# A cross-attention and mixture-of-experts layer: how the router's choice of four is computed, and when its steps are issued

## The chip, the core and the metric

The kernel runs on one core of one Trainium2 chip. The core has five engines that each take their instructions in order from a queue of their own and wait for each other by semaphores: TensorE (PE in the profile, with PEld for its weight loads), VectorE (DVE), ScalarE (ACT), GpSimd (POOL) and SyncE (SP, which here only issues DMA transfers). The metric is the device time of one execution in microseconds. The kernel before took 1699.78 us, the median of three runs that went from 1699.21 to 1702.81 us.

## What is computed

A layer on 4 sequences of 512 tokens of width 512: layer norm, cross-attention to a context of 1601 rows (257 image rows and 1344 text rows, two softmaxes, 16 heads), a residual sum, a second layer norm, and a feed-forward part with 32 experts and a shared expert. The change lies in the feed-forward part. Cut to what matters:

```python
scores = sigmoid(x @ router_w.T)                     # T = 2048 tokens, 32 experts
sc = scores + e_bias
group_scores = top_k(sc.reshape(T, 8, 4), 2)[0].sum(-1)
gidx = top_k(group_scores, 3)[1]                     # three of eight groups
masked = where(expert's group is chosen, sc, 0.0)
topk_idx = top_k(masked, 4)[1]                       # the choice of four
topk_w = 2.5 * scores[topk_idx] / (sum of the four + 1e-20)

# each expert takes its first C = 80 tokens, in order of the token number
Y[e] = (silu(Xp[e] @ W_gate[e]) * (Xp[e] @ W_up[e])) @ W_down[e]    # Xp[e]: 80 gathered rows
out[slots_token] += Y * slots_w
shared = silu(x @ shared_gate.T) * (x @ shared_up.T) @ shared_down.T
result = x + out + shared
```

All arrays are float32.

## The kernel before

The order of the work on every engine is written out by hand: a planner has no part in it. An engine that reaches an instruction whose inputs are not there stands still, with all that is queued behind it.

**Stages.** The loop over the four batches `b` computes keys, queries and values, then the attention by groups of four heads (`c` from 0 to 3) and key tiles (`t` from 0 to 12). Inside a batch first come the keys, sixteen chunks of four matmuls (`keys`, L718), then a written-out list with the last scores and the residual steps of the batch before (L793), then the attention. `residual` (L441) projects the attention's output, adds x, normalizes, transposes, and computes the router's logits of 128 tokens.

After the last batch comes the shared expert (`shared`, L938): 32 units of mostly 3.4 us of TensorE work (`gate`, `up` and `down` of 128 x 512 results). Here `residual` of the last batch is spread over units 8 to 15 (`side`). Then come the 32 experts (loop at L1118): `gate_up(e)`, `turn(e + 2)`, `down(e - 1)`, with eight units of the shared expert strewn between, and at the end eight last units.

**The router.** `routing(b, space)` (L511) returns a list of small steps for the 512 tokens of one batch, nearly all on DVE, with 128 tokens on the partitions and four such rows side by side. `carve` lays its small arrays out in a scratch tile `space`. The steps are: the sigmoid on ACT (or by exp, for batches 0 and 1), the bias, the two largest of each group, the rank of each group, the masked scores `cand`; then four rounds that each find the largest left, settle ties by the smaller expert number with the help of `rev` (32, 31, ... 1), and take the hit out (L583 to L597); then the weights and their DMA to `xw_d` (L605), behind the normed rows that the experts gather. Then `ranks` (L611) transposes the 0/1 choice to 32 x 512 on PE, and DVE adds it to `merged`, where each chosen token's key is larger the smaller its number. Nineteen steps of `search` (ten MAX8 and nine match-replaces on 32 x 592 elements, L625 to L629) keep the 80 largest keys of each expert in `best`, over all batches.

**When the steps are issued.** For batches 0 and 1 the steps go two per key tile of the last head group of the next batch (L879 to L886), then seven per key chunk of the batch after it (L789), and the search one per key tile (L877). For batches 2 and 3 they are dealt out in the shared-expert stage by `deal(i)` (L1085): after unit `i`, as many steps as keep a running sum `spent` (0.8 for a search step, 0.3 for another) under `(i - 1) * SHARE`. Batch 2 has its scratch in a tile of its own, `rp` (L1072), batch 3 in a tile that the attention has left (L1105), from unit 16 on (`ready`).

**From the router to the experts.** Before unit 30, the last but one, all steps that are left are issued, and then `tokens` (L929): two DVE steps turn `best` into token numbers (`past`), PE transposes them (L935), DVE casts them to `tok` (L936). Then six `gather(e)` (L1013, `AHEAD`) are issued on POOL's queue: indirect DMAs of 80 rows each into `xp`, a ring of seven buffers. In the expert loop `down(e - 1)` issues its scatter (L1050), which adds to `out`, and then `gather(e + 5)` follows on the same queue. `turn(e)` transposes the gathered rows on PE (L1026) and copies them on DVE (L1028). The expert's weights come by SP's queue into rings of six buffers (`expert_weights`, L919): one expert after every fourth unit, then each as a buffer comes free. SP's queue also holds the loads of x rows for `residual` (L168), of rows for `down` of the shared expert (L977) and all writes.

PSUM is a ring of eight banks, each taken in turn by `psum`.

Of the kernel before, what the change touches and what calls it, by code (L numbers as in the profile page):

```python
# [109 lines left out]
def body(ctx, tc, a, ident, mhalf, logits, x1_d, xw_d, xnT_d, den_d, rec_d, out):  # L110
# [383 lines left out]

    rt = pool("rt", 1)
    e_b = rt.tile([P, E], F32, name="e_b")
    rev = rt.tile([P, 1, E], F32, name="rev")
    below = rt.tile([P, NG, NG], F32, name="below")

    merged = rt.tile([E, CAP + L], F32, name="merged")  # L500
# [1 line left out]

    def routing_constants():
        nc.scalar.dma_start(e_b, a["e_bias"].partition_broadcast(P))
        nc.gpsimd.iota(rev[:, 0, :], [[-1, E]], base=E, channel_multiplier=0, allow_small_or_imprecise_dtypes=True)
        nc.gpsimd.memset(below, 1.0)

        nc.gpsimd.affine_select(below, below, [[1, NG], [-1, NG]], ALU.is_gt, 0.0, base=0, channel_multiplier=0)
        nc.vector.memset(best, 0.0)

    def routing(b, space, by_exp=False):  # L511


        tt, ts, tr = nc.vector.tensor_tensor, nc.vector.tensor_scalar, nc.vector.tensor_reduce
        lo = b * NQ
        taken = []

        def carve(*shape):

            n = NQ  # L520
            for d in shape:
                n *= d
            at = sum(taken)
            taken.append(n)
            names = " ".join("abc"[:len(shape)])
            return space[:, at:at + n].rearrange(
                f"p (t {names}) -> p t {names}", t=NQ, **dict(zip("abc", shape))
            )

        lg = logits[:, lo:lo + NQ, :]  # L530

        both = carve(4 * E)
        first_half, second_half = space[:, :2 * NQ * E], space[:, 2 * NQ * E:4 * NQ * E]
        gt, eq = (x.rearrange("p (t a b) -> p t a b", t=NQ, a=NG) for x in (first_half, second_half))
        cand, hit, sel, chosen = (
            space[:, k * NQ * E:(k + 1) * NQ * E].rearrange("p (t e) -> p t e", t=NQ) for k in range(4)
        )
        sc, sb = carve(E), carve(E)
        m = [carve(NG) for _ in range(4)]
        gs, rank, top = carve(NG), carve(NG), carve(1)  # L540
        g = sb.rearrange("p t (g k) -> p t g k", k=EG)
        one = gs.unsqueeze(3).to_broadcast([P, NQ, NG, NG])
        oth = gs.unsqueeze(2).to_broadcast([P, NQ, NG, NG])
        rv = rev.to_broadcast([P, NQ, E])
        before = below.unsqueeze(1).to_broadcast([P, NQ, NG, NG])

        def wide_(x):
            return x.to_broadcast([P, NQ, E])

        if by_exp:  # L550

            work = [
                lambda: nc.scalar.activation(sc, lg, AF.Exp, scale=-1.0),
                lambda: ts(sc, sc, 1.0, None, ALU.add),
                lambda: nc.vector.reciprocal(sc, sc),
            ]
        else:
            work = [lambda: nc.scalar.activation(sc, lg, AF.Sigmoid)]
        work += [
            lambda: tt(sb, sc, e_b.unsqueeze(1).to_broadcast([P, NQ, E]), ALU.add),  # L560

            lambda: tt(m[0], g[:, :, :, 0], g[:, :, :, 1], ALU.max),
            lambda: tt(m[1], g[:, :, :, 0], g[:, :, :, 1], ALU.min),
            lambda: tt(m[2], g[:, :, :, 2], g[:, :, :, 3], ALU.max),
            lambda: tt(m[3], g[:, :, :, 2], g[:, :, :, 3], ALU.min),
            lambda: tt(m[1], m[1], m[3], ALU.max),
            lambda: tt(m[3], m[0], m[2], ALU.min),
            lambda: tt(m[0], m[0], m[2], ALU.max),
            lambda: tt(m[1], m[1], m[3], ALU.max),
            lambda: tt(gs, m[0], m[1], ALU.add),  # L570

            lambda: tt(gt, oth, one, ALU.is_gt),
            lambda: tt(eq, oth, one, ALU.is_equal),
            lambda: tt(eq, eq, before, ALU.mult),
            lambda: tt(gt, gt, eq, ALU.add),
            lambda: tr(rank, gt, AX.X, ALU.add),
            lambda: ts(rank, rank, float(TKG), None, ALU.is_lt),
            lambda: tt(
                cand.rearrange("p t (g k) -> p t g k", k=EG), g, rank.unsqueeze(3).to_broadcast([P, NQ, NG, EG]), ALU.mult
            ),  # L580
        ]

        for k in range(TOPK):  # L583
            into = sel if k else chosen
            work += [
                lambda: tr(top[:, :, 0], cand, AX.X, ALU.max),
                lambda: tt(hit, cand, wide_(top), ALU.is_equal),
                lambda: tt(hit, hit, rv, ALU.mult),
                lambda: tr(top[:, :, 0], hit, AX.X, ALU.max),
                lambda into=into: tt(into, hit, wide_(top), ALU.is_equal),  # L590
            ]
            if k:
                work.append(lambda: tt(chosen, chosen, sel, ALU.add))
            if k < TOPK - 1:
                work.append(
                    lambda into=into: nc.vector.scalar_tensor_tensor(cand, into, -BIG, cand, ALU.mult, ALU.add)
                )  # L597
        work += [
            lambda: tt(sb, chosen, sc, ALU.mult),
            lambda: tr(top[:, :, 0], sb, AX.X, ALU.add),  # L600
            lambda: ts(top, top, 1e-20, None, ALU.add),
            lambda: nc.vector.reciprocal(top, top),
            lambda: ts(top, top, SCALE_ROUTE, None, ALU.mult),
            lambda: tt(sb, sb, wide_(top), ALU.mult),
            lambda: nc.sync.dma_start(  # L605
                xw_d[lo * P:(lo + NQ) * P, D:].rearrange("(t p) e -> p t e", p=P), sb
            ),
        ]
        key = merged[:, CAP:]

        def ranks():  # L611
            ps = psum()
            for i in range(NQ):
                nc.tensor.transpose(ps[:E, i * P:(i + 1) * P], chosen[:, i, :], ident)  # L614
            nc.vector.scalar_tensor_tensor(key, ps[:E, :], float(T), key, ALU.mult, ALU.add)

        work += [
            lambda: nc.gpsimd.iota(
                key, [[-1, L]], base=T - b * L, channel_multiplier=0, allow_small_or_imprecise_dtypes=True
            ),  # L620
            lambda: nc.vector.tensor_copy(merged[:, :CAP], best),
            ranks,
        ]
        search = []
        for j in range(CAP // 8):  # L625
            at = best[:, 8 * j:8 * j + 8]
            search.append(lambda at=at: nc.vector.max(at, merged))
            if j < CAP // 8 - 1:
                search.append(lambda at=at: nc.vector.match_replace(merged, at, merged, 0.0))  # L629
        return work, search  # L630
# [292 lines left out]
            nc.sync.dma_start(t, a[name][e])  # L923
            weights.setdefault(e, []).append(t)

    SHARE = 2.4
    AHEAD, WEIGHTS = 6, 6

    def tokens():  # L929

        past = ew.tile([E, CAP], F32, name="past", bufs=1)
        nc.vector.tensor_scalar(past, best, T + 0.5, float(T), ALU.is_gt, ALU.mult)
        nc.vector.scalar_tensor_tensor(past, past, float(T), best, ALU.add, ALU.subtract)
        ps = psum()
        nc.tensor.transpose(ps[:CAP, :E], past, ident[:E, :E])  # L935
        nc.vector.tensor_copy(tok, ps[:CAP, :E])  # L936
# [73 lines left out]
    def expert_parts():  # L1010
        weights, xps, xpTs, hs = {}, {}, {}, {}

        def gather(e):  # L1013
            xps[e] = ew.tile([CAP, D + E], F32, name="xp", bufs=AHEAD + 1)
            nc.gpsimd.indirect_dma_start(
                out=xps[e][:, :],
                out_offset=None,
# [51 lines left out]
    early.close()  # L1069
    wgp = pool("wgp", WEIGHTS, side="right", reuse_waits="tile")  # L1070
    ew = pool("ew", 3, side="right", reuse_waits="tile")
    rp = pool("rp", 1, side="right", reuse_waits="tile")  # L1072
    tok = ew.tile([CAP, E], I32, name="tok", bufs=1)
    weights, gather, turn, gate_up, down = expert_parts()
    rest = [residual(B - 1, qt, aoT_last, lambda: wo) for qt in range(NQ)]
    first, second = sum(routing(B - 2, rp.tile([P, 1024], F32, name="space")), []), None
    O_AT = 8
    side = {}
    for qt in range(NQ):
        for i, f in enumerate(rest[qt]):  # L1080
            side.setdefault(O_AT + qt + i, []).append(f)
    ready = O_AT + NQ + 4
    spent = 0.0

    def deal(i):  # L1085

        nonlocal spent
        while spent < (i - 1) * SHARE and (first or second):
            todo = first or second
            spent += 0.8 if len(todo) < 2 * CAP // 8 else 0.3  # L1090
            todo.pop(0)()

    for i, u in enumerate(units):
        if i < 2:
            continue
        if i == len(units) - 2:
            for f in first + second:
                f()
            first, second = [], []
            tokens()  # L1100
            for e in range(AHEAD):
                gather(e)
        if i == ready:

            space = mid.tile([P, 2, L], F32, name="rb")  # L1105
            second = sum(routing(B - 1, space.rearrange("p k t -> p (k t)")), [])
            deal(i)
        u()
        for f in side.get(i, ()):
            f()  # L1110
# [66 lines left out]
```

## Time and profile before

| | us |
|---|---|
| median of three runs | 1699.78 |
| the profiled execution, its own time | 1697.61 |
| its span, from the first to the last instruction | 1695.9 |
| first unit of the shared expert starts on PE | 1324.4 |
| `tokens` on PE (L935) | 1452.0 |
| first expert's matmuls start | 1460.5 |
| last eight units start | 1664.5 |
| record of the last matmul ends | 1692.1 |

The granted clock of PE is 1.00 in all forty slices of the page. The groups of the routing that matter, from the timelines:

| step | on | us for one |
|---|---|---|
| 128x128 elements, as L586 to L596 | DVE | 0.29, starts 0.32 apart |
| 128x32 elements, as L562 to L570 | DVE | 0.19 to 0.22 |
| MAX8 of 32x592, L627 | DVE | 0.76 |
| match-replace of 32x592, L629, with its value load | DVE | 0.75 + 0.07 |
| transposes of a choice, four, L614 | PE | 0.6 together |
| a gather, L1015 | POOL | 0.93, starts 1.21 apart; lands 3.0 to 3.3 later |
| a scatter, L1050 | POOL | 1.42; lands 6.0 later (median) |

How to read the profile: busy times are sums of instruction records. Records of matmuls overlap, since matmuls are pipelined and their ends are modelled. In timelines each line has start, duration, engine, line, operation, output and inputs, and in square brackets how long the engine stood idle before, and what released it. In a list of waits each line has the waiting line, what released it, the total in us, how often, and the longest.

### The profile page before, as it was taken

Reading aid. Unit: us, or ns where it says so; the run is one execution under the profiler, and the core shown is the slowest. Engines: PE = TensorE matmul, PEld = TensorE weight load, DVE = VectorE, ACT = ScalarE, POOL = GpSimd, SP = SyncE. Lnnn points to the kernel's source line nnn. Section 1 sums busy time; section 2 is a strip of 40 time slices with the busy share of each in tenths; the row PEclk is TensorE's granted clock in tenths of the full one; section 3 lists DMA queues with packets and bytes.
Section 4 is the critical chain, followed back from the end, with each engine's and each line's share of the span. In section 5 each row is a group of like instructions: output and inputs, shape, how many; then the busy total and the mean of one; then the engine's idle time right before and its main releaser. Section 6 shows DMA issues by size and latency. Waiting matters only on the chain. (4 is left out here: it accounts for less than half of the span.)

```text
span 1695.9 us, 29514 instructions
## 1 busy us (share of the span) xinstructions
PE 1683.7 (99%) x11773; PEld 885.0 (52%) x11773; DVE 981.1 (58%) x2024; ACT 643.1 (38%) x1370; POOL 868.4 (51%) x614
## 2 busy tenths in 40 slices
PE   9999999999999999999999999999999999999999
PEld 5554444446544444465444445654443344677774
DVE  4765554857655549776665597766655777211111
ACT  2135456611355566114555651145556401111110
POOL 3246977332569764336697643366884210233331
PEclk9999999999999999999999999999999999999999
DMA  7000000321100103120010041210001365599964
GB/s 234 1 1 1 27 27 2 114 67 63 38 1 27 27 2 123 59 72 29 2 27 27 2 147 34 81 44 2 14 15 64 132 206 188 176 287 297 306 179 117
DMA packets 68969, 138.40 MB, mean 82 GB/s; under 512 B 16224, under 2 KB 28640, under 8 KB 66784
## 3 DMA queue, kind: packets, MB, share of 16 engines
q1 hardware_dynamic: 62704, 124.11, 22.1%
q0 software_dynamic: 5120, 10.82, 3.1%
q8 instruction: 93, 1.52, 0.4%
q10 hardware_dynamic: 1008, 1.59, 0.3%
q14 instruction: 44, 0.36, 0.1%
HBM read 113.68 MB, written 22.81 MB: 80 GB/s over the span
## 5 line engine op out<-in xcount | busy, mean ns | idle before, releaser
L372 ACT ACTIVATE pT<-ps 128x512 f32<-128x512 f32 (+1 forms) x832 | 429.7, 603 | 345.9 <-PE ps L371 337.8
L334 DVE TENSOR_REDUCE mx<-ps 128x1 f32<-128x512 f32 (+1 forms) x576 | 331.3, 617 | 265.1 <-PE ps L320 265.1
L387 POOL TENSOR_TENSOR acc<-acc,pT 128x1024 f32<-128x1024 f32 x192 | 445.7, 2360 | 3.0 <-ACT pT L372 2.6
L290 PEld LDWEIGHTS ps<-v_w,cT 128*128 128x128 f32 (+1 forms) x1408 | 168.9, 186 | 102.2 <-DVE mx L334 56.1
L379 PE MATMUL po<-pT,v 128*32 128x512 f32 (+2 forms) x1792 | 222.3, 603 | 0.0
L371 PE MATMUL ps<-qT,kT 32*128 32x512 f32 (+1 forms) x1664 | 213.7, 587 | 0.0
L320 PE MATMUL ps<-kT,qT 32*128 32x512 f32 (+1 forms) x1536 | 206.4, 549 | 0.0
L290 PE MATMUL ps<-v_w,cT 128*128 128x128 f32 (+1 forms) x1408 | 197.7, 284 | 0.0
L231 PE MATMUL ps<-cT,wk 128*128 128x512 f32 (+1 forms) x384 | 154.0, 545 | 0.2 <-DMA wk<-in_k_w 0.2
L308 DVE TENSOR_REDUCE mx<-ps 128x1 f32<-128x512 f32 (+2 forms) x256 | 128.2, 565 | 6.4 <-PE ps L305 6.4
L1050 POOL DMA_INDIRECT out<-y,tok x32 | 45.4, 1420 | 133.2 <-DMA out<-y,tok 72.5
L368 PEld LDWEIGHTS <-pick 32*128 32x128 bf16 (+1 forms) x832 | 21.6, 91 | 165.8 <-issue 164.0
L231 PEld LDWEIGHTS ps<-cT,wk 128*128 128x128 f32 x384 | 69.6, 190 | 70.5 <-issue 55.5
L298 ACT COPY v<-ps 128x128 f32<-128x128 f32 (+1 forms) x208 | 59.7, 287 | 117.7 <-PE ps L290 117.3
L238 POOL TENSOR_TENSOR sq_k<-sq_k,sq 128x512 f32<-128x512 f32 (+2 forms) x48 | 49.6, 1034 | 104.5 <-ACT sq L235 104.1
L1040 DVE TENSOR_TENSOR ehT<-ehT,ps 128x160 f32<-128x160 f32 x32 | 10.3, 321 | 158.3 <-ACT ehT L1039 144.1
L394 POOL TENSOR_TENSOR acc<-pT 128x1024 f32<-128x1024 f32 x24 | 56.1, 2360 | 86.8 <-ACT pT L372 54.3
L387 POOL TENSOR_TENSOR pT<-pT 65x1024 f32<-65x1024 f32 x24 | 56.0, 2355 | 86.8 <-PE po L379 78.1
L320 PEld LDWEIGHTS ps<-kT,qT 32*128 32x128 f32 x1536 | 82.1, 183 | 31.0 <-issue 10.1
L387 DVE TENSOR_TENSOR acc<-acc,pT 128x1024 f32<-128x1024 f32 (+1 forms) x72 | 96.7, 1391 | 2.1 <-ACT pT L372 2.1
L379 PEld LDWEIGHTS po<-pT,v 128*32 128x32 f32 (+2 forms) x1792 | 34.9, 107 | 118.6 <-issue 109.3
L368 PE MATMUL ps<-mT,pick 32*128 32x512 bf16 (+1 forms) x832 | 82.5, 385 | 2.5 <-ACT mT L359 2.5
(244 smaller groups left out, 2194.5 us busy)
## 6 DMA issues: line engine op xcount, KB each, us to landing
W_gate<-in_W_gate SPq DMA_DIRECT2D x32, 512.0 KB
W_up<-in_W_up SPq DMA_DIRECT2D x32, 512.0 KB
W_down<-in_W_down SPq DMA_DIRECT2D x32, 512.0 KB
rb<-rec_d SPq DMA_DIRECT2D x64, 128.0 KB
xt<-in_x SPq DMA_DIRECT2D x30, 256.0 KB
cT<-in_ctxT SPq DMA_DIRECT2D x7, 1024.0 KB
wki<-in_k_img_w SPq DMA_DIRECT2D x4, 1024.0 KB
wo<-in_o_w SPq DMA_DIRECT2D x4, 1024.0 KB
```

Of the source, the lines that this page charges most:

```text
L231: nc.tensor.matmul(ps[:, :n], lhsT=wt[:, k, c * P:(c + 1) * P], rhs=xT[:, k, to], start=k == 0, stop=k == NC - 1)
L290: nc.tensor.matmul(ps[lo:hi, :], lhsT=cTs[bl][:, k, at:at + hi - lo], rhs=ws[bl == NB - 1][:, k, c * P:(c + 1) * P], start=k == 0, stop=k ...
L298: nc.scalar.copy(v[:n, t, :], ps[:n])
L308: nc.vector.tensor_reduce(mx[:, qt, g, bl:bl + 1], ps[:, :n], AX.X, ALU.max, negate=True)
L320: nc.tensor.matmul(ps[:, j * n:(j + 1) * n], lhsT=qT[r:r + HD, c, q * P:(q + 1) * P], rhs=kT[r:r + HD, c, k0:k0 + n], start=True, stop=True,)
L334: nc.vector.tensor_reduce(mx[:, qt, g, i:i + 1], ps[:, :m], AX.X, ALU.max, negate=True)
L368: nc.tensor.matmul(ps[:n], lhsT=pick[r:r + HD, kind(t), :n], rhs=mT[r:r + HD, :], start=True, stop=False)
L371: nc.tensor.matmul(ps[:n], lhsT=kT[r:r + HD, c, t * P:t * P + n], rhs=qT[r:r + HD, c, :], start=False, stop=True)
L372: nc.scalar.activation(pT[:n, g, :], ps[:n], AF.Exp)
L379: nc.tensor.matmul(po[r:r + HD, :], lhsT=v[rows, t, r:r + HD], rhs=pT[rows, g, :], start=start, stop=stop)
L387: (nc.vector if idle else nc.gpsimd).tensor_tensor(to[rows, h, :], to[rows, h, :], pT[rows, h, :], ALU.add)
L394: (nc.vector if idle else nc.gpsimd).tensor_tensor(acc[:, h, :], pTs[0][:, h, :], pTs[1][:, h, :], ALU.add)
```

## The change

1. The four rounds of the choice are replaced. `cand` now lies in rows of 36 (`filled`), the last four of which hold a very low number. For each of the four rows of tokens a MAX8 gives the eight largest of 32; the lower four of these are overwritten by the same low number; a match-replace takes the eight values out of the 36, each once; and a comparison of `cand` with what is left gives the choice. `rev` and its iota are gone.
2. `SHARE` is 2.7 instead of 2.4. In `deal`, when the next step is `ranks` (20 steps left), the dealing stops for this part, once for each batch, so that `ranks` comes with the next part. At unit 16 the running sum is set forward instead of dealing at once.
3. All steps that are left, and the two DVE steps of the slots, are issued before unit 29 (`kept_tokens`); the transpose, the cast and the gathers stay before unit 30.
4. `AHEAD` is 8 instead of 6, and `xp` has `AHEAD` buffers (8) instead of `AHEAD + 1` (7).
5. The scratch of batch 2 is the first buffer of the ring of `W_down`; the tile `rp` is gone.

```diff
--- before.py
+++ after.py
@@ -494,7 +494,6 @@
 
     rt = pool("rt", 1)
     e_b = rt.tile([P, E], F32, name="e_b")
-    rev = rt.tile([P, 1, E], F32, name="rev")
     below = rt.tile([P, NG, NG], F32, name="below")
 
     merged = rt.tile([E, CAP + L], F32, name="merged")
@@ -502,7 +501,6 @@
 
     def routing_constants():
         nc.scalar.dma_start(e_b, a["e_bias"].partition_broadcast(P))
-        nc.gpsimd.iota(rev[:, 0, :], [[-1, E]], base=E, channel_multiplier=0, allow_small_or_imprecise_dtypes=True)
         nc.gpsimd.memset(below, 1.0)
 
         nc.gpsimd.affine_select(below, below, [[1, NG], [-1, NG]], ALU.is_gt, 0.0, base=0, channel_multiplier=0)
@@ -532,16 +530,19 @@
         both = carve(4 * E)
         first_half, second_half = space[:, :2 * NQ * E], space[:, 2 * NQ * E:4 * NQ * E]
         gt, eq = (x.rearrange("p (t a b) -> p t a b", t=NQ, a=NG) for x in (first_half, second_half))
-        cand, hit, sel, chosen = (
-            space[:, k * NQ * E:(k + 1) * NQ * E].rearrange("p (t e) -> p t e", t=NQ) for k in range(4)
+
+        row_ = E + 8 - TOPK
+        filled, rest_ = (
+            space[:, k * NQ * row_:(k + 1) * NQ * row_].rearrange("p (t e) -> p t e", t=NQ) for k in range(2)
         )
+        cand = filled[:, :, :E]
+        chosen = space[:, 2 * NQ * row_:2 * NQ * row_ + NQ * E].rearrange("p (t e) -> p t e", t=NQ)
         sc, sb = carve(E), carve(E)
         m = [carve(NG) for _ in range(4)]
-        gs, rank, top = carve(NG), carve(NG), carve(1)
+        gs, rank, top, largest8 = carve(NG), carve(NG), carve(1), carve(8)
         g = sb.rearrange("p t (g k) -> p t g k", k=EG)
         one = gs.unsqueeze(3).to_broadcast([P, NQ, NG, NG])
         oth = gs.unsqueeze(2).to_broadcast([P, NQ, NG, NG])
-        rv = rev.to_broadcast([P, NQ, E])
         before = below.unsqueeze(1).to_broadcast([P, NQ, NG, NG])
 
         def wide_(x):
@@ -575,26 +576,20 @@
             lambda: tt(gt, gt, eq, ALU.add),
             lambda: tr(rank, gt, AX.X, ALU.add),
             lambda: ts(rank, rank, float(TKG), None, ALU.is_lt),
+            lambda: nc.vector.memset(filled[:, :, E:], -BIG / 2),
             lambda: tt(
                 cand.rearrange("p t (g k) -> p t g k", k=EG), g, rank.unsqueeze(3).to_broadcast([P, NQ, NG, EG]), ALU.mult
             ),
         ]
 
-        for k in range(TOPK):
-            into = sel if k else chosen
-            work += [
-                lambda: tr(top[:, :, 0], cand, AX.X, ALU.max),
-                lambda: tt(hit, cand, wide_(top), ALU.is_equal),
-                lambda: tt(hit, hit, rv, ALU.mult),
-                lambda: tr(top[:, :, 0], hit, AX.X, ALU.max),
-                lambda into=into: tt(into, hit, wide_(top), ALU.is_equal),
-            ]
-            if k:
-                work.append(lambda: tt(chosen, chosen, sel, ALU.add))
-            if k < TOPK - 1:
-                work.append(
-                    lambda into=into: nc.vector.scalar_tensor_tensor(cand, into, -BIG, cand, ALU.mult, ALU.add)
-                )
+
+        work += [lambda t=t: nc.vector.max(largest8[:, t, :], cand[:, t, :]) for t in range(NQ)]
+        work += [lambda: nc.vector.memset(largest8[:, :, TOPK:], -BIG / 2)]
+        work += [
+            lambda t=t: nc.vector.match_replace(rest_[:, t, :], largest8[:, t, :], filled[:, t, :], -BIG)
+            for t in range(NQ)
+        ]
+        work += [lambda: tt(chosen, cand, rest_[:, :, :E], ALU.is_gt)]
         work += [
             lambda: tt(sb, chosen, sc, ALU.mult),
             lambda: tr(top[:, :, 0], sb, AX.X, ALU.add),
@@ -923,14 +918,18 @@
             nc.sync.dma_start(t, a[name][e])
             weights.setdefault(e, []).append(t)
 
-    SHARE = 2.4
-    AHEAD, WEIGHTS = 6, 6
-
-    def tokens():
+    SHARE = 2.7
+    AHEAD, WEIGHTS = 8, 6
+
+    def kept_tokens():
 
         past = ew.tile([E, CAP], F32, name="past", bufs=1)
         nc.vector.tensor_scalar(past, best, T + 0.5, float(T), ALU.is_gt, ALU.mult)
         nc.vector.scalar_tensor_tensor(past, past, float(T), best, ALU.add, ALU.subtract)
+        return past
+
+    def tokens(past):
+
         ps = psum()
         nc.tensor.transpose(ps[:CAP, :E], past, ident[:E, :E])
         nc.vector.tensor_copy(tok, ps[:CAP, :E])
@@ -1011,7 +1010,7 @@
         weights, xps, xpTs, hs = {}, {}, {}, {}
 
         def gather(e):
-            xps[e] = ew.tile([CAP, D + E], F32, name="xp", bufs=AHEAD + 1)
+            xps[e] = ew.tile([CAP, D + E], F32, name="xp", bufs=AHEAD)
             nc.gpsimd.indirect_dma_start(
                 out=xps[e][:, :],
                 out_offset=None,
@@ -1069,42 +1068,50 @@
     early.close()
     wgp = pool("wgp", WEIGHTS, side="right", reuse_waits="tile")
     ew = pool("ew", 3, side="right", reuse_waits="tile")
-    rp = pool("rp", 1, side="right", reuse_waits="tile")
     tok = ew.tile([CAP, E], I32, name="tok", bufs=1)
     weights, gather, turn, gate_up, down = expert_parts()
     rest = [residual(B - 1, qt, aoT_last, lambda: wo) for qt in range(NQ)]
-    first, second = sum(routing(B - 2, rp.tile([P, 1024], F32, name="space")), []), None
+
+    space = wgp.tile([P, NI, D], F32, name="W_down", tag="W_down")
+    first, second = sum(routing(B - 2, space.rearrange("p n d -> p (n d)")), []), None
     O_AT = 8
     side = {}
     for qt in range(NQ):
         for i, f in enumerate(rest[qt]):
             side.setdefault(O_AT + qt + i, []).append(f)
     ready = O_AT + NQ + 4
-    spent = 0.0
+    spent, waited = 0.0, None
+    N_SEARCH = 2 * (CAP // 8) - 1
 
     def deal(i):
 
-        nonlocal spent
+        nonlocal spent, waited
         while spent < (i - 1) * SHARE and (first or second):
             todo = first or second
+            if len(todo) == N_SEARCH + 1 and waited is not todo:
+
+                waited = todo
+                break
             spent += 0.8 if len(todo) < 2 * CAP // 8 else 0.3
             todo.pop(0)()
 
     for i, u in enumerate(units):
         if i < 2:
             continue
-        if i == len(units) - 2:
+        if i == len(units) - 3:
             for f in first + second:
                 f()
             first, second = [], []
-            tokens()
+            past = kept_tokens()
+        if i == len(units) - 2:
+            tokens(past)
             for e in range(AHEAD):
                 gather(e)
         if i == ready:
 
             space = mid.tile([P, 2, L], F32, name="rb")
             second = sum(routing(B - 1, space.rearrange("p k t -> p (k t)")), [])
-            deal(i)
+            spent = (i - 1) * SHARE
         u()
         for f in side.get(i, ()):
             f()
```

## The prediction

> **What bounds the kernel now.** I read the head of the page first, then the list of what TensorE (PE) waited for, then the timelines of PE and VectorE (DVE) around the longest of those waits that lies near the change.
>
> ```profile
> span 1695.9 us, 29514 instructions
> PE 1683.7 (99%) x11773; PEld 885.0 (52%) x11773; DVE 981.1 (58%) x2024; ACT 643.1 (38%) x1370; POOL 868.4 (51%) x614
> ```
>
> PE has 1683.7 us of records in 1695.9 us, so 12.2 us at most stand open. The list of PE's waits names 8.3 us of them; nearly all the rest is the tail behind the last matmul (its record ends at 1692.1).
>
> ```profile
> PE ps L368 <- ACT mT L359: 2.5, 4, 0.6
> PE ps L468 <- DVE xn L220: 1.8, 3, 0.6
> PE ps L639 <- POOL ones L200: 1.2, 1, 1.2
> PE ps L935 <- DVE past L933: 1.2, 1, 1.2
> PE ps L225 <- DVE xpT L1028: 0.7, 1, 0.7
> PE ps L614 <- DVE v L593: 0.7, 2, 0.3
> PE ps L231 <- DMA wk<-in_k_w: 0.2, 1, 0.2
> ```
>
> Columns: waiting line, releaser, total us, times, longest. Only three have to do with the change: L614 (transposes of the choice in `ranks`, twice 0.3), L935 (transpose of the slots in `tokens`, 1.2) and L1028 (behind the first gathers, 0.7). L468 and L368 sit in the residual lists and at the changes of head group, where no routing step of this diff is queued.
>
> ```profile
> 1447.14 3.60 PE L225 MATMUL ps<-xT,shared_up 128*128 128x512 f32 x8
> 1451.95 0.22 PE L935 MATMUL ps<-ident,past 32*80 32x32 f32 x1 [1.21 <-DVE past L933]
> 1452.10 3.70 PE L225 MATMUL ps<-xT,shared_gate 128*128 128x512 f32 x8
> ...
> 1459.08 0.72 PE L1026 MATMUL ps<-ident,xp 80*128 80x80 f32 x8
> ```
>
> ```profile
> 1446.17 0.77 DVE L627 MAX8 best<-merged 32x8 f32<-32x592 f32 x1
> 1450.85 0.69 DVE L971 TENSOR_TENSOR hT<-hT,ps 128x512 f32<-128x512 f32 x1 [3.91 <-PE ps L225]
> 1451.45 0.18 DVE L932 TENSOR_SCALAR past<-best 32x80 f32<-32x80 f32 x1
> 1451.67 0.23 DVE L933 SCALAR_TENSOR_TENSOR past<-past,best 32x80 f32<-32x80 f32 x1
> ```
>
> The reader is to see that the search was over at 1446.9, and that DVE then stood idle 3.91 us: `past` is not late for want of time, but because it is queued behind the eviction (L971) of the unit that PE has just ended.
>
> Is PE held back where its records hide it? In the attention stage the same step of PE comes with and without a search instruction on DVE:
>
> ```profile
> 788.03 0.39 PE L368 MATMUL ps<-mT,pick 32*128 32x512 bf16 x4
> 792.50 0.39 PE L368 MATMUL ps<-mT,pick 32*128 32x512 bf16 x4
> ```
>
> ```profile
> 911.16 0.39 PE L368 MATMUL ps<-mT,pick 32*128 32x512 bf16 x4
> 915.69 0.40 PE L368 MATMUL ps<-mT,pick 32*128 32x512 bf16 x4
> ```
>
> The first step takes 4.47 us with 2.48 us of reduces and a 0.76 us MAX8 on DVE, the second 4.53 us with 2.48 us and a 0.34 us reciprocal. More DVE work does not make the step longer, so PE sets its own pace there. In the expert stage all of the 20 us stretches from 1480 to 1680 show PE busy for 20.00 us.
>
> [...]
>
> **The change, part by part.**
>
> *Choice by the eight largest.* Each of four routings loses 26 DVE instructions (rounds of 6, 7, 7, 6), which start 0.32 us apart in the routing of the last batch (1410.35, 1410.67): 8.3 us. It gains 4 MAX8, 4 match-replaces with a value load each, 2 memsets and a comparison. The trace has no MAX8 of 32 elements. From above: the 592-element rows, 0.76 for MAX8 and 0.08+0.75 for the replace, plus 0.6 for the other three: 7.0 us. From below: the 128x32 tensor ops at 0.19, times 11, and four loads at 0.07: 2.4 us. I take 2.4, being nearest in size. So DVE is relieved of 1.3 to 5.9 us per routing, 5 to 23 us in all; DVE is 58% busy and off the path, so the direct worth is zero.
>
> *Ranks in batches 0 and 1.* Routing goes in groups of seven per key chunk, after 22 items in the attention before. With 56 items `ranks` fell into the fifth chunk, just behind the last L593, and PE waited 0.33 us (692.69) and 0.34 us (1029.18). With 41 items it falls into the third chunk, its choice being item 31 in the second, a full chunk (3.43 us) earlier. Both waits go: 0.67 us. DVE's next step there waits for an iota on POOL, which moves up before one addition of squares (1.27 us); POOL was idle 1.8 to 4.3 us between those, so nothing is late.
>
> *Spreading with 2.7 a part, ranks held one part.* In the shared-expert stage the routing of batch 2 now ends its search at part 11 and that of batch 3 at part 26 (38 items, one part held, 19 search steps), against 14 and 28. L614 caused no wait here before, and the choice is made two parts ahead, so none arises. ACT's sigmoid of batch 3 moves behind one more gate; with two table loads it takes 2.9 us where ACT had 6.27 us idle.
>
> *Slots one part earlier.* L932/L933 now stand ahead of the eviction, and their search ends near 1446. L935 can follow its unit directly: units start 3.43 us apart (1443.71, 1447.14), so at 1450.57 instead of 1451.95: 1.4 us by starts, 1.2 by the idle row. I take 1.3.
>
> What is late next? `tok` (L936) stays behind L971, so the first gather starts 0.7 us earlier (1452.0 for 1452.71) while its transposes come 1.3 us earlier: 5.8 us between them instead of 6.4. Gathers land in 3.0 to 3.3 us, and the second starts 1.5 us after the first, which leaves 0.7 to 1.3 us. The 0.7 at L1028 stays, since its copy is behind the same eviction as before.
>
> *Eight gathers.* Two more cost POOL 2 x 1.2 us directly after the first six, in an 11.1 us idle stretch before its first scatter. Worth nothing: no transposition of a gathered tile (L1026) waited for DMA. `xp` has one buffer less than the distance would ask for, but the buffer and the scatter before it in POOL's queue wait for the same ACT instruction (L1049).
>
> *Routing space in a W_down buffer; one iota of 32 columns dropped.* Nothing: the sixth W_down is loaded at part 24, long after the space is free, and PE never waited for weights.
>
> Sum: 0.67 + 1.3 = 2.0 us, bounds 1.9 to 2.1 if nothing else moves. The profiled execution took 1697.6 us for a span of 1695.9; it should come to a span of 1693.9. The median of the runs shown, 1699.8, lies 2.2 us above the profiled one; the forecast is 1699.8 - 2.0 = 1697.8.
>
> **The rivals.**
>
> *The relief reaches further.* If the freed DVE also took away L468 (1.8), L368 (2.5) and L1028 (0.7), all 6.9 us of inner waits go: 1692.9. For it: those waits end on DVE or right behind it. Against: each sits where DVE's queue is the same before and after. Chance 0.13.
>
> *The gain comes back at the gathers.* If eight gathers in one queue land as slowly as the scatters do (6.0 us), the second is there 1.5 + 6.0 = 7.5 us after the first starts and is needed after 6.2: 1.3 us are lost again, 1699.1. For it: the margin shrinks. Against: 3.0 to 3.3 us is the whole spread of 32 gathers, also under full weight traffic. Chance 0.08.
>
> *Slower: the search of batch 3 ends too late.* In SP's queue the write of the routing weights now stands before expert 4's weights, which were issued at 1405 and now at about 1421 (DVE reaches L604 near 1420.7). The rows for the next down units (L977) are queued behind these 1.5 MB. At the 255 to 269 GB/s seen at 1431 to 1439 that is 5.9 us, and a bare row load takes 2.8 (1424.48 to 1427.29): rows at 1430.6 for a unit that ends at 1426.5, so DVE stands 4.1 us with `ranks` and 19 search steps behind. I count `past` done at 1446.5 without this, so 4.1 us of slack: it decides from there on. If single DVE steps also stretch as they did at 1345 to 1356 (1.24, 0.92, 1.31, 1.11 for 0.29: 3.4 us in all), PE stalls 3.4 us at L935 instead of 1.4: +2.0 - 0.7, 1701.1. Against: at 1407 to 1415 loads ran at 407 to 416 GB/s, which halves the delay. Chance 0.10.
>
> *No effect,* as in a wait that only changes its name: 1699.8, chance 0.03.
>
> **How the numbers follow.** The forecast has 0.66; its own range is 1696.8 to 1699.0, since three runs of one kernel span 1699.2 to 1702.8. The range given, 1695.4 to 1701.3, takes in the gathers, the slower rival and the nearer half of the far-reaching one. From no change a measurement here can tell about 0.2%, 3.4 us. Faster by more: most of the first rival and a low set of runs, 0.14. Slower by more: the far end of the third rival or a cost that no row shows, 0.08. Within: 0.78.
>
> **What would show it.** Right: PE's list without L614 and without the slots' transpose, L468, L368 and L1028 unchanged, DVE's busy time down by some 20 us, PE's by nothing, the span down by 2. Wrong: a new PE wait at the transposes of gathered tiles (second rival), a wait for `past` with DVE waiting for x1r rows ahead of it (third), or a changed PE step in the attention stage.

## The result, and the profile after

| | before | after |
|---|---|---|
| median, us (11 runs of each, in turns) | 1699.12 | 1695.23 |
| lowest to highest, us | 1697.54 to 1702.81 | 1695.11 to 1695.91 |
| the profiled execution, its own time | 1697.61 | 1695.23 |
| its span | 1695.9 | 1693.5 |

The ratio is 0.9978, with an interval of 0.997 to 0.9986: 3.9 us by the medians, where 2.0 were forecast. The time is faster by a little more than 0.2%, and it lies just under the lower end of the range given. The table says something else too: the lowest runs differ by only 2.4 us, as do the two profiled executions, but the runs of the kernel before are strewn over 5.3 us and those of the changed one over 0.8. So there are two differences to explain.

The head of the page after:

```profile
span 1693.5 us, 29471 instructions
PE 1682.8 (99%) x11773; PEld 884.5 (52%) x11773; DVE 955.6 (56%) x1980; ACT 643.1 (38%) x1370; POOL 865.8 (51%) x613
```

DVE has lost 25.5 us and 44 instructions, PE nearly nothing. The list of PE's waits after (waiting line, releaser, total us, times, longest):

```profile
PE ps L368 <- ACT mT L359: 2.5, 4, 0.6
PE ps L468 <- DVE xn L220: 1.8, 3, 0.6
PE ps L634 <- POOL ones L200: 1.2, 1, 1.2
PE ps L225 <- DVE xpT L1027: 0.7, 1, 0.7
PE ps L231 <- DMA wk<-in_k_w: 0.6, 1, 0.6
```

The transposes of the choice and of the slots have gone from it; L368, L468 and the wait behind the first gathers (now L1027) stand as before. PE's timeline around the slots, after (start, duration, instruction):

```profile
1446.05 3.60 PE L225 MATMUL ps<-xT,shared_up 128*128 128x512 f32 x8
1449.58 0.22 PE L934 MATMUL ps<-ident,past 32*80 32x32 f32 x1
1449.73 3.70 PE L225 MATMUL ps<-xT,shared_gate 128*128 128x512 f32 x8
...
1456.70 0.72 PE L1025 MATMUL ps<-ident,xp 80*128 80x80 f32 x8
1458.12 2.01 PE L225 MATMUL ps<-xpT,W_gate 128*128 128x80 f32 x16 [0.70 <-DVE xpT L1027]
```

And DVE's timeline over the same stretch:

```profile
1444.81 0.77 DVE L622 MAX8 best<-merged 32x8 f32<-32x592 f32 x1
1445.50 0.66 DVE L988 TENSOR_TENSOR x1r<-x1r,ps 128x512 f32<-128x512 f32 x1
1446.09 0.18 DVE L927 TENSOR_SCALAR past<-best 32x80 f32<-32x80 f32 x1
1446.31 0.23 DVE L928 SCALAR_TENSOR_TENSOR past<-past,best 32x80 f32<-32x80 f32 x1
1449.75 0.69 DVE L970 TENSOR_TENSOR hT<-hT,ps 128x512 f32<-128x512 f32 x1 [3.22 <-PE ps L225]
```

`past` is done at 1446.5, 3.0 us before PE comes to it, and it stands in front of the eviction (L970), not behind it. The transpose follows its unit at 1449.58 with no bracket.

Setting the starts of the same PE instructions of the two traces side by side (after minus before, without the transposes of the choice, which have moved) gives where the 2.4 us of the profiled executions come from. The difference is -0.08 us ahead of the first `ranks` and -0.47 behind it, -0.42 ahead of the second and -0.81 behind it, -1.11 from one step at 1145 on, the same at the first shared unit (1323.34 for 1324.44), and -2.37 behind the slots (first expert's matmuls at 1458.12 for 1460.49). From there to the end the two run in step.

The 0.28 us at 1145 stand in no list of waits. ACT's exponentials (L372) start later there behind the same matmuls, first before, then after:

```profile
1144.14 2.07 ACT L372 ACTIVATE pT<-ps 128x512 f32<-128x512 f32 x4 [2.58 <-PE ps L371]
```

```profile
1143.03 2.07 ACT L372 ACTIVATE pT<-ps 128x512 f32<-128x512 f32 x4 [2.30 <-PE ps L371]
```

PE's L320 matmuls in that step take 1.61 us before and 1.33 after. All eight traces of kernels with the old choice have the 2.58, all six with the new one the 2.30. So this gain comes with the new choice; what holds ACT there is not shown.

Eight gathers change nothing between these two executions. The other part, the spread, can't be seen in them.

### The profile page after: what moved, and what is told of

Same layout as the page of the kernel before. It is cut to its first block, busy times and chain, and to the rows that moved or that the text cites. A ratio compares the mean times of both kernels' runs of the same rounds, so it can differ in the third digit from the quotient of the medians.

```text
span 1693.5 us, 29471 instructions
## 1 busy us (share of the span) xinstructions
PE 1682.8 (99%) x11773; PEld 884.5 (52%) x11773; DVE 955.6 (56%) x1980; ACT 643.1 (38%) x1370; POOL 865.8 (51%) x613
## 5 line engine op out<-in xcount | busy, mean ns | idle before, releaser
L372 ACT ACTIVATE pT<-ps 128x512 f32<-128x512 f32 (+1 forms) x832 | 429.7, 603 | 345.7 <-PE ps L371 335.3
L320 PE MATMUL ps<-kT,qT 32*128 32x512 f32 (+1 forms) x1536 | 206.2, 549 | 0.0
L231 PE MATMUL ps<-cT,wk 128*128 128x512 f32 (+1 forms) x384 | 154.1, 546 | 0.6 <-DMA wk<-in_k_w 0.6
L368 PEld LDWEIGHTS <-pick 32*128 32x128 bf16 (+1 forms) x832 | 21.7, 91 | 165.8 <-issue 164.0
L231 PEld LDWEIGHTS ps<-cT,wk 128*128 128x128 f32 x384 | 69.5, 190 | 70.8 <-issue 53.9
L320 PEld LDWEIGHTS ps<-kT,qT 32*128 32x128 f32 x1536 | 82.0, 183 | 30.8 <-issue 10.1
L368 PE MATMUL ps<-mT,pick 32*128 32x512 bf16 (+1 forms) x832 | 82.6, 385 | 2.5 <-ACT mT L359 2.5
```

Of the source, the lines that this page charges most:

```text
L231: nc.tensor.matmul(ps[:, :n], lhsT=wt[:, k, c * P:(c + 1) * P], rhs=xT[:, k, to], start=k == 0, stop=k == NC - 1)
L320: nc.tensor.matmul(ps[:, j * n:(j + 1) * n], lhsT=qT[r:r + HD, c, q * P:(q + 1) * P], rhs=kT[r:r + HD, c, k0:k0 + n], start=True, stop=True,)
L368: nc.tensor.matmul(ps[:n], lhsT=pick[r:r + HD, kind(t), :n], rhs=mT[r:r + HD, :], start=True, stop=False)
L372: nc.scalar.activation(pT[:n, g, :], ps[:n], AF.Exp)
```

## Experiments

Each was timed in turns with the kernel before, except the three looks. The expectations are as written ahead of the runs.

### The kernel before, again, and the changed one beside it

No edit. Is the spread a property of the kernel, or of the chip that the runs were made on?

> The kernel before, unchanged. Theory A (the change takes 2.4 us out of PE's queue, and the wide spread of the runs before, 1697.5 to 1702.8, belongs to chips and hours): on one chip the copy lies within 0.1% of the kernel before, and its spans spread no more than those of the changed kernel. Theory B (the kernel before has a stall that comes in some executions only, and the change takes it out): spans of this copy spread by 2 to 5 us at a granted clock of 1.0, while the changed kernel's stay within 1 us.

> The changed kernel again, on the same chip as the copy of the one before. Theory A: the medians differ by 2.0 to 2.6 us, as the two traces do. Theory B: the medians differ by 3 to 4 us and the fastest runs by 2.4.

Before, under its new label: median 1697.64, 1697.29 to 1703.22 in 12 runs. The same kernel in 35 more runs on that chip: median 1698.81, 1697.39 to 1703.06. After: 1695.17, 1695.05 to 1695.79, ratio 0.9978 [0.997, 0.9987]. On one chip, in turns, the kernel before is strewn over 5 us and the changed one is not. Two sets of one kernel have medians 1.2 us apart with nearly the same lowest time, so the median tells how many of the executions came late. With all five sets of this study, 51 of 98 lie above 1698.5, and the median of the 98 is 1698.65.

### The slots one part earlier, alone

The edit, cut to the calls (`tokens` is split as in the changed kernel):

```diff
-        if i == len(units) - 2:
+        if i == len(units) - 3:
             for f in first + second:
                 f()
             first, second = [], []
-            tokens()
+            past = kept_tokens()
+        if i == len(units) - 2:
+            tokens(past)
```

> The kernel before with one part of the change alone: the rest of the search and the two slot steps before unit 29. Predicted: L935 starts right behind its unit, 1.3 us less span, and both waits at L614 (0.33, 0.34) stay. If the executions with a late end come from the slots (a form of theory B), this one alone also takes the spread away and gains 2 us or more in the median; by theory A it gains 1.3.

Median 1696.66 (1696.13 to 1701.76), ratio 0.9991 [0.9982, 1.0]. The lowest run is 1.2 us under that of the kernel before on this chip (1697.29), which is the wait at L935. The spread stays: 3 of the 11 runs lie more than 1 us above the lowest.

### The new choice, alone

The routing of the changed kernel, with all else as before.

```diff
-        for k in range(TOPK):
...
+        work += [lambda t=t: nc.vector.max(largest8[:, t, :], cand[:, t, :]) for t in range(NQ)]
```

> The kernel before with the new choice alone (MAX8 and match-replace, no rev), old share, old slots, six gathers. Predicted: both waits at L614 go, 0.7 us less span, L935 keeps its 1.2 us; DVE's busy time falls by 20 to 26 us. If freed DVE time is worth more than the waits named, the span falls by more than 1 us.

Median 1696.89 (1696.70 to 1698.89), ratio 0.999 [0.9981, 0.9999]; lowest run 0.6 under before's. 3 of the 11 runs lie more than 1 us above it. From its list of PE's waits:

```profile
PE ps L930 <- DVE past L928: 1.2, 1, 1.2
PE ps L225 <- DVE xpT L1023: 0.7, 1, 0.7
PE ps L609 <- DVE rb L592: 0.2, 1, 0.2
```

The reader is to see that the two waits of 0.33 and 0.34 at `ranks` are gone, and that a third, which was not there before, has come at the `ranks` of batch 3 (`rb` is its scratch). Set beside the trace before as above, PE gains 0.39 us at each of the two `ranks` and 0.28 at 1145, and loses 0.35 at the `ranks` of batch 3. DVE's busy time is 955.7 us: the relief of 25 us gave PE nothing beyond these.

### Eight gathers, alone

```diff
-    AHEAD, WEIGHTS = 6, 6
+    AHEAD, WEIGHTS = 8, 6
-            xps[e] = ew.tile([CAP, D + E], F32, name="xp", bufs=AHEAD + 1)
+            xps[e] = ew.tile([CAP, D + E], F32, name="xp", bufs=AHEAD)
-    first, second = sum(routing(B - 2, rp.tile([P, 1024], F32, name="space")), []), None
+    space = wgp.tile([P, NI, D], F32, name="W_down", tag="W_down")
+    first, second = sum(routing(B - 2, space.rearrange("p n d -> p (n d)")), []), None
```

> The kernel before with eight gathers ahead and the routing scratch in the W_down ring, and nothing else of the change. Theory G (the executions of 1699 to 1703 us of the kernel before have PE waiting for gathered rows in the expert stage): the spread goes, all within 1 us of 1697.5. Theory X (they have PE waiting in the shared-expert stage, for rows or weights that SP's queue holds behind the routing's write) and theory S (the search ends too late for the slots): the spread stays, 1697.4 to 1702 or so, and the fastest stay at 1697.4.

Median 1697.78, 1697.49 to 1698.12 in 11 runs; before beside it 1698.28, 1697.41 to 1702.19 in 15, 7 of them over 1698.5. Ratio 0.9991 [0.9982, 1.0]. The lowest time is that of the kernel before, the late executions are gone. The edit also moves the scratch of batch 2, but a run below that keeps this move and goes back to six gathers has late executions again; so it is the gathers. In all, 53 runs of five kernels with eight gathers lie within 0.9 us of the lowest of their kernel.

### Three looks at the kernel before

No edit, one profile each, to catch a late execution in the trace.

> The kernel before, for a trace of a late execution, over 1698.5 us (more than half of its runs are). Theory G: PE waits at L1026, or at L225 in the expert loop, for DMA or DVE after 1460. Theory X: new PE waits between 1334 and 1450 with DVE or POOL waiting for xt or x1r. Theory S: the wait at L935 grows from 1.2 us by all of the lateness. If the execution is not late, it shows the waits known.

> The same as the look before it: another chance of a late execution, read the same way.

> The same as the two looks before it: another chance of a late execution, read the same way.

Times 1699.21, 1697.61 and 1698.97; spans 1697.5, 1695.9 and 1697.3. The second is the execution that the prediction saw, wait for wait but for the 0.2 us at its start (L231). The other two have one line more in their lists of PE's waits, here of the first look:

```profile
PE ps L1026 <- DMA xp<-xw_d,tok: 1.3, 1, 1.3
```

In its timeline of PE it is the transposes of expert 24:

```profile
1602.97 1.95 PE L225 MATMUL ps<-xpT,W_up 128*128 128x80 f32 x16
1606.26 0.47 PE L1026 MATMUL ps<-ident,xp 80*128 80x80 f32 x4 [1.35 <-DMA xp<-xw_d,tok]
```

POOL's timeline shows when those rows were asked for:

```profile
1597.20 1.42 POOL L1050 DMA_INDIRECT out<-y,tok  x1 [5.13 <-ACT y L1049]
1598.92 0.93 POOL L1015 DMA_INDIRECT xp<-xw_d,tok  x1 [0.30 <-issue]
1603.94 1.42 POOL L1050 DMA_INDIRECT out<-y,tok  x1 [4.09 <-DMA out<-y,tok]
```

The gather of expert 24 went out at 1598.92, right behind the scatter of expert 18, and PE wanted its rows 6.0 us later; they came 7.3 us later. Of the landings, the source view of that line says:

```profile
DMA to landing us min/median/max: 2.9/5.5/7.4
```

This is not 3.0 to 3.3 us. The trace that the prediction read has landings for only a part of its transfers (for its weight loads none at all): of the 32 gathers two have one, those of experts 0 and 2, both issued ahead of the first scatter. In the first look all 32 have one, and there the first six took 2.9 to 3.2 us, those from expert 7 on 3.1 to 7.4. The bracket `DMA out<-y,tok` at the scatters shows the rest: a scatter waits for the landing of the one before (4.09 us in the last row of POOL above). Following each `y` from its readiness to its scatter, the scatters' lag grows from 0.3 us at expert 0 to 4 to 9 us at experts 9 to 24 of the first look. And as `gather(e + 5)` stands behind the scatter of `e - 1` on the same queue, a gather's lead over its transposes shrinks from 15.0 us (expert 6) to 6 to 11 us from expert 17 on. A lead of 6 us and landings of up to 7.4 us meet in some executions and not in others. In the changed kernel, POOL and PE have for the same expert:

```profile
1583.11 0.93 POOL L1014 DMA_INDIRECT xp<-xw_d,tok  x1 [0.30 <-issue]
```

```profile
1602.30 0.44 PE L1025 MATMUL ps<-ident,xp 80*128 80x80 f32 x4
```

The lead is 19.2 us, though the landings are no shorter (source view of the gathers, after):

```profile
DMA to landing us min/median/max: 2.9/5.6/7.4
```

### Fewer gathers: in the changed kernel six, in the kernel before five

```diff
-    AHEAD, WEIGHTS = 8, 6
+    AHEAD, WEIGHTS = 6, 6
-            xps[e] = ew.tile([CAP, D + E], F32, name="xp", bufs=AHEAD)
+            xps[e] = ew.tile([CAP, D + E], F32, name="xp", bufs=AHEAD + 1)
```

> The changed kernel with six gathers ahead and seven buffers, as before. Theory G (the late executions are PE waiting at L1026 for a gather that stood on POOL behind a late scatter): the fastest runs stay at 1695.1, but the spread of 2 to 6 us comes back, and the median lies 0.5 to 2 us above the changed kernel's. If the other parts of the change took the spread away, all runs stay within 1 us of 1695.2.

Median 1695.27, 1695.11 to 1699.10, ratio 0.9982 [0.9973, 0.9991]. The spread is back, but in 3 of 11 runs (1697.19, 1697.21, 1699.10), so the median moves by 0.1 us only: more was expected. The leads in its trace are 7.5 to 11 us from expert 17 on. The kernels with the slots alone and the choice alone had 3 late runs of 11 too, where the kernel before has 51 of 98 more than 1 us above the lowest of their set. Why these are late less often, with nearly the same leads, was not found.

```diff
-    AHEAD, WEIGHTS = 6, 6
+    AHEAD, WEIGHTS = 5, 6
```

> The kernel before with five gathers ahead (six buffers). In its trace gathers were issued 7 to 10 us before their transposes in the second half of the experts and landed up to 7.4 us later in the traces that show it; one expert less ahead is 5.5 to 9 us less. Theory G: every run is late, PE waits at L1026 for most later experts and falls to the pace of the scatters (6.9 us against 6.4): 8 to 12 us slower, 1705 to 1710. If the lead of the gathers did not matter, 1697.4 to 1702 as before.

Median 1708.93 (1706.73 to 1710.06, 5 runs), ratio 1.0055 [1.004, 1.0071], span 1707.5. One gather less costs 10.7 us, and the first line of its list of PE's waits says where:

```profile
PE ps L1026 <- DMA xp<-xw_d,tok: 6.7, 4, 2.7
```

That is 6.7 of the 11.6 us by which the span grew; some of the rest is in the last section.

### The changed kernel with the old dealing

```diff
-    SHARE = 2.7
+    SHARE = 2.4
-            if len(todo) == N_SEARCH + 1 and waited is not todo:
-                waited = todo
-                break
-            spent = (i - 1) * SHARE
+            deal(i)
```

> The changed kernel with the old share of 2.4, without the part that is held before the ranks, and dealing at unit 16 at once. The kernel with the new choice alone had 0.2 us of PE waiting at the ranks of batch 3 for the choice. Expected: this wait comes back, 0.2 us slower than the changed kernel, with no more spread. If the new dealing is worth more, over 0.5 us slower.

Median 1695.65 (1695.39 to 1696.12), ratio 0.9979 [0.997, 0.9988]; 0.3 us above the changed kernel by the lowest runs. The third wait, seen above with the new choice alone, is in its list of waits:

```profile
PE ps L609 <- DVE rb L592: 0.2, 1, 0.2
```

With the shorter choice and the old dealing, `ranks` of batch 3 comes right behind its last DVE steps. The new dealing, as a whole, is worth 0.3 us by the lowest runs and 0.36 by the starts of PE's instructions at that place, so it repairs what the new choice had brought. The held part was not run apart from the larger share; that the wait stands at `ranks` speaks for it.

### The first two copies of gathered rows on ACT

```diff
-            nc.vector.tensor_copy(xpTs[e], px)
+            (nc.scalar.copy if e < 2 else nc.vector.tensor_copy)(xpTs[e], px)
```

> The changed kernel with the first two copies of gathered rows (L1027) on ACT, which is idle there, instead of behind the eviction on DVE. The wait of 0.70 us at the first expert's matmuls shrinks to 0.1 to 0.3; 0.4 to 0.6 us faster than the changed kernel, 1694.6 to 1694.8. If the wait is the transposes' own time, nothing changes.

Median 1694.68 (1694.52 to 1695.37), ratio 0.9978 [0.9968, 0.9988] against before. PE's timeline at the first expert:

```profile
1456.62 0.72 PE L1025 MATMUL ps<-ident,xp 80*128 80x80 f32 x8
1457.58 2.01 PE L225 MATMUL ps<-xpT,W_gate 128*128 128x80 f32 x16 [0.24 <-issue]
```

The 0.70 us at L1027 has become 0.24: what was late was the copy in DVE's queue behind an eviction, not the gather. It is the quickest version of the study, some 0.5 us below the changed kernel in another set of runs.

## Why the prediction was right and wrong

*Choice by the eight largest: right at the two `ranks`, luck in its total.* The new choice alone takes off 0.6 us in the lowest runs, against 0.67 counted for `ranks`. But by the starts the two gave 0.78, and two amounts that no term held nearly cancel: 0.28 won at 1145 and 0.35 lost at the `ranks` of batch 3. A MAX8 of 32 elements takes 0.18 us, a match-replace of 36 takes 0.18 and its value load 0.08, which is the lower bound (0.19 and 0.07) that was taken. Their records overlap (four MAX8 take 0.47 us together), so the relief of DVE, 25.5 us, is above the 5 to 23 counted.

*Slots one part earlier: right.* 1.2 us by the lowest runs of that edit alone, 1.3 counted; no stall in front of `past`'s transpose.

*"None arises", at the spread with 2.7 a part: right in the changed kernel, for a reason that was not seen.* The prediction took the shared-expert stage as it was before, where L614 had no wait, and put the new dealing at nothing. The new choice by itself brings a wait there, 0.35 us by the starts, and the new dealing removes it.

*The wait behind the first gathers: right.* It stays at 0.7, and its cause, the place of the copy, holds in the run with ACT.

*"Eight gathers ... Worth nothing": the step that failed.* It rested on "no transposition of a gathered tile (L1026) waited for DMA" and on landings of 3.0 to 3.3 us as "the whole spread of 32 gathers". Both were read from one execution that had no such wait, the landings from two gathers of the 32. The second look shows the same execution; the first and third show 1.3 us at L1026, and single runs of the kernel before are up to 5.9 us above its lowest. Eight gathers alone remove this. They are worth nothing in the lowest runs. The medians of 1699.12 and 1695.23 lie 1.6 and 0.1 us above the lowest runs of their set: so 1.5 us of the 3.9 are late executions that are gone. The eight gathers are enough for that, but not all of it is theirs: the changed kernel with six has a median only 0.1 us higher, as its late executions are rarer, for a cause that stays open. Nor has any execution later than 1699.2 us a trace.

The same slip is in the last term of the sum. The 2.2 us between the profiled execution (1697.6) and the median of the runs shown (1699.8) were carried over to the forecast as if every execution had them. They were late executions, which this change removes. The three runs were also a high draw: the 98 runs of the kernel before have a median 1.1 us lower. The span was forecast at 1693.9 and is 1693.5.

*The whole.* Lowest against lowest, on one chip, 2.24 us (1697.29 to 1695.05); by the starts in the two profiled executions 2.38: `ranks` 0.78, the step at 1145 0.28, slots 1.28. Another 1.5 us of the median are the late executions.

*The rivals.* "The gain comes back at the gathers" expected slow landings for the first gathers. In the changed kernel the first seven land in 2.9 to 3.3 us; only over all 32 are gathers as slow as scatters (medians 5.6 and 5.8 us). The first gather of the changed kernel starts at 1450.85, and PE takes its rows at 1456.70 with no wait. The slower rival's delay did arise, at half its size. Weights of an expert now stand ahead of the rows for the next down unit (issued at 1420.85), and DVE stood for that unit's sum:

```profile
1427.13 0.69 DVE L988 TENSOR_TENSOR x1r<-x1r,ps 128x512 f32<-128x512 f32 x1 [4.50 <-issue]
```

PE had gone on to its next instruction at 1425.01, so DVE was 2.1 us late, against 4.1 counted. The profile names no releaser here (in the kernel before, the same line names the rows' DMA); that it was the rows is argued from the order of the queue. For a loss this rival needed `past` later than 1449.6; it was done at 1446.5. That is the very time that the prediction counted without this delay, so the agreement is luck. The relief that reaches further did not come: L468 and L368 are untouched.

## What to carry to other kernels

Runs of a kernel that scatter upward from a firm lowest time can have an intermittent wait in them, as here (1.3 us at L1026): look for it in the trace of a late execution before a transfer is called hidden, for a profiled execution near the lowest time may show none. For each transfer in a ring, compare the lead from issue to use, late in the loop, with the longest landing and not the median; a queue that also holds transfers which wait for each other eats that lead from one turn to the next (here from 15.0 us at expert 6 down to between 6 and 11 us from expert 17 on, against landings of up to 7.4 us). When one stage of steps is shortened, look at what now follows its end directly.

## What was not expected of the hardware

In the kernel with five gathers, two of PE's four waits at L1026 cost more than their length. The windows of PE in steps of 1 us (stretch, length, busy us with instructions, granted clock, share of the DMA engines, GB/s) around the longest, 2.74 us, which ended at 1565.52, are:

```profile
1564.00:1565.00 1.00, 0.00 (x0) 1.00 1.01 273
1565.00:1566.00 1.00, 0.48 (x5) 1.00 0.94 373
1566.00:1567.00 1.00, 1.00 (x3) 0.96 1.12 309
1567.00:1568.00 1.00, 1.00 (x2) 0.50 0.81 163
1568.00:1569.00 1.00, 1.00 (x3) 0.50 0.39 130
1569.00:1570.00 1.00, 1.00 (x3) 0.50 0.48 113
1570.00:1571.00 1.00, 1.00 (x4) 0.83 0.97 373
1571.00:1572.00 1.00, 1.00 (x4) 1.00 0.54 74
```

Some 1.5 us after PE had begun again, its granted clock stood at 0.50 for over 3 us. In PE's timeline the matmuls behind that wait, 1.88 us elsewhere, take 2.53:

```profile
1565.52 0.47 PE L1026 MATMUL ps<-ident,xp 80*128 80x80 f32 x4 [2.74 <-DMA xp<-xw_d,tok]
1565.82 2.53 PE L1045 MATMUL ps<-W_down,ehT 128*80 128x512 f32 x4
```

Summed over the stretches, (1 - clock) is 1.7 us for this wait and as much again behind one of 1.56 us at 1614.54, which are 3.4 us besides the 6.7 of the waits themselves. The starts of PE's instructions agree: from these transposes to the `gate` matmuls of the next expert, over the same work, it takes 7.15 us behind each of the two, and 5.45 behind the wait of 1.11 us before 1515.27. That shorter wait left the clock at 1.00, and behind it, as behind those of 1.3 us in the looks, the L1045 matmuls take 1.88 us. What sets the two longer waits apart, their length or something else, these runs do not show.
